# One scan over two channel halves in a selective-scan layer: a carry column between the halves, two two-bank decay buffers, one side bank

## The chip, the core and the metric

The kernel runs on one core of one Trainium2 chip. The metric is the device time of that core in microseconds, from the first to the last instruction. Five engines work from queues of their own: TensorE (PE in the profile, with PEld for its weight loads), VectorE (DVE), ScalarE (ACT), GpSimd (POOL) and SyncE (SP), which here only issues transfers. [...] a bank holds 512 float32 columns.

## The reference, cut to what matters

The program has two layers. The second (a Fourier attention block) is untouched by the change. The first is a two-dimensional selective scan: for each of 4 images of 48x48 pixels with 256 inner channels, four directions k run over the 2304 pixels, and each channel d has 16 states:

```python
def step(h, inp):
    dt_l, u_l, B_l, C_l = inp
    dA = jnp.exp(dt_l[..., None] * A)
    h = h * dA + (dt_l * u_l)[..., None] * B_l[:, :, None, :]
    y = jnp.einsum('bkdn,bkn->bkd', h, C_l)
    return (h, y)
```

Directions 2 and 3 run the pixels backwards. Afterwards come a sum over the directions, a layer norm over the channels, a multiplication by silu(z) and an output projection.

## The kernel before

Channels lie on the 128 partitions, so the 256 channels are two halves f = 0, 1 side by side in the free dimension. Pixels are cut into chunks of 480 (four of them, and one of 384) for each direction: 4 images x 4 directions x 5 chunks = 80 chunks. For every chunk the 16 states are 16 steps, 1280 steps in all. A step is spread over the engines:

```python
NX = 112
LC = 480
CHUNKS = [(s, min(LC, L - s)) for s in range(0, L, LC)]
...
three = ctx.enter_context(tc.tile_pool(name="l0_three", bufs=3))          # db, h, hc, cbc
ps_s = ctx.enter_context(tc.tile_pool(name="l0_pss", bufs=2, space=PSUM))  # side work
ps_b = ctx.enter_context(tc.tile_pool(name="l0_psb", bufs=1, space=PSUM))  # B of a state, spread
ps_a = ctx.enter_context(tc.tile_pool(name="l0_psa", bufs=3, space=PSUM))  # decays da
ps_y = ctx.enter_context(tc.tile_pool(name="l0_psy", bufs=1, space=PSUM))  # two sums yp
...
def drive_pool(u):          # every fourth step: the input term db on GpSimd
    u.db = three.tile([128, NF, LC], F32, tag="db", ...)
    if i % 4 == POOLS:
        nc.gpsimd.tensor_mul(u.db[:, :, 0:n], c.du[:, :, 0:n], u.bbc[...])
def spread(u):              # the other steps: TensorE spreads B over the partitions ...
    u.pb = ps_b.tile([128, 512], F32, tag="pb", ...)
    nc.tensor.matmul(u.pb[:, 0:n], pick[:, i : i + 1].to_broadcast([NX, 128]), c.bs[:, 0:n], ...)
def drive_in(u):            # ... and VectorE multiplies
    nc.vector.tensor_mul(u.db[:, :, 0:n], c.du[:, :, 0:n], u.pb[:, None, 0:n].to_broadcast(...))
def decay(u):               # ScalarE: exp(dt * A), one PSUM bank for each half
    for f in range(NF):
        da = ps_a.tile([128, 512], F32, tag="da", ...)
        nc.scalar.activation(da[:, 0:n], c.dt[:, f, 0:n], AF.Exp, scale=a_neg[:, q, i : i + 1])
        u.da.append(da)
def scan(u):                # VectorE: the recurrence, one scan for each half
    for f in range(NF):
        init = 0.0 if c.first else carry[:, i, f : f + 1]
        ...
        nc.vector.tensor_tensor_scan(ha, aa, ba, init, ALU.mult, ALU.add)
def read_out(u):            # GpSimd: times C
    nc.gpsimd.tensor_mul(u.hc[:, :, 0:n], u.h[:, :, 0:n], u.cbc.to_broadcast([128, NF, n]))
def carry_on(u):            # ScalarE: last column of both halves, for the next chunk
    nc.scalar.copy(carry[:, u.i], u.h[:, :, 0 if u.c.k >= 2 else u.c.n - 1])
def sum_up(u):              # TensorE: the sum over states, by the identity, in PSUM
    for f in range(NF):
        nc.tensor.matmul(c.yp[f][:, 0:n], ident, u.hc[:, f, 0:n], ...)
...
LAGS = (
    (0, fetch), (3, drive_pool), (4, drive_in), (5, scan), (4, decay), (5, read_out), (6, carry_on),
    (3, spread), (7, sum_up),
)
```

LAGS says how many steps after its fetch each stage of a step is recorded, and in which order within one advance. After each advance one piece of side work is recorded: the next direction's projections (`project`: TensorE into a side bank, ScalarE out of it), the next image's convolution (`front`) and the tail of finished chunks (`back`). A scheduling layer then orders each engine's queue; the queues are fixed when the program is built. `back` before the change, cut:

```python
pz = []
for f in range(NF):
    p = side(f"pz{t}_{f}")
    nc.tensor.matmul(like(p[:, 0:n], 1), w[...], xs, start=True, stop=True)
    pz.append(p)
for f in range(NF):
    nc.scalar.activation(z[:, f, 0:n], pz[f][:, 0:n], AF.Silu, bias=wb[...])
yield
nc.gpsimd.tensor_mul(ys, ys, z[:, :, 0:n])
yield
po = side(f"po{t}")
...   # two matmuls into po
yield
pr = side(f"pr{t}")
...   # three matmuls into pr
yield
nc.vector.tensor_mul(xo[:, 0:n], po[:, 0:n], rs[:, 0:n])
yield
nc.vector.tensor_add(xo[:, 0:n], xo[:, 0:n], pr[:, 0:n])
```

Of the kernel before, what the change touches and what calls it, by code (L numbers as in the profile page):

```python
# [22 lines left out]
D = 256  # L23
NF = D // 128
N = 16
R = 8
K = 4
NX = 112
NH = 32

LC = 480
# [4 lines left out]
def layer0(ctx, tc, io, x1_dram):  # L36
# [17 lines left out]

# [13 lines left out]

    w_xp = const.tile([128, K, NF, NX], F32, name="w_xp")
    nc.gpsimd.memset(w_xp, 0.0)  # L70
# [35 lines left out]
    def side(name):  # L106
        return ps_s.tile([128, 512], F32, tag="pp", name=name)
# [7 lines left out]
    def like(ap, k):  # L115

        return ap if k % 2 == 0 else ap.rearrange("p (w h) -> p w h", h=T)
# [73 lines left out]
    def project(b, k, chunks, xc):  # L191
# [5 lines left out]
        for c in chunks:  # L197
# [49 lines left out]
    def back(b, s, n, yb, x, w, wb):  # L247


        t = f"{b}_{s}"  # L250
        xs = at(x, 1, s, n)[:, 0]
        pm = side(f"pm{t}")
        for f in range(NF):
            nc.tensor.matmul(pm[:, 0:n], lnmat, yb[:, f, 0:n], start=(f == 0), stop=(f == NF - 1))
        yield
        ys = yb[:, :, 0:n]
        nc.vector.tensor_sub(ys, ys, pm[:, None, 0:n].to_broadcast([128, NF, n]))
        yield
# [12 lines left out]
        pz = []  # L271
        for f in range(NF):
            p = side(f"pz{t}_{f}")
            nc.tensor.matmul(
                like(p[:, 0:n], 1), w[:, D + f * 128 : D + (f + 1) * 128], xs, start=True, stop=True
            )
# [9 lines left out]
        yield  # L286
        pr = side(f"pr{t}")
# [4 lines left out]
        nc.vector.tensor_mul(xo[:, 0:n], po[:, 0:n], rs[:, 0:n])  # L292
        yield
# [5 lines left out]
    carry = const.tile([128, N, NF], F32, name="carry")  # L299

    class Chunk:


        def __init__(self, b, k, s, n, first, number, im):
            self.b, self.k, self.s, self.n, self.first, self.number, self.im = b, k, s, n, first, number, im
            self.t = f"{b}_{k}_{s}"

    class Step:
# [15 lines left out]
    def drive_pool(u):  # L324

        c, i, n = u.c, u.i, u.c.n
        u.db = three.tile([128, NF, LC], F32, tag="db", name=f"db{c.t}_{i}")
        if i % 4 == POOLS:
            nc.gpsimd.tensor_mul(u.db[:, :, 0:n], c.du[:, :, 0:n], u.bbc[:, :, 0:n].to_broadcast([128, NF, n]))  # L329

    def spread(u):

# [10 lines left out]
    def drive_in(u):  # L343
        c, i, n = u.c, u.i, u.c.n
        if i % 4 != POOLS:
            nc.vector.tensor_mul(  # L346
                u.db[:, :, 0:n], c.du[:, :, 0:n], u.pb[:, None, 0:n].to_broadcast([128, NF, n])
            )

    def decay(u):  # L350
        c, i, n = u.c, u.i, u.c.n
        u.da = []
        for f in range(NF):
            q = c.k * NF + f
            da = ps_a.tile([128, 512], F32, tag="da", name=f"da{c.t}_{i}_{f}")
            nc.scalar.activation(da[:, 0:n], c.dt[:, f, 0:n], AF.Exp, scale=a_neg[:, q, i : i + 1])  # L356
            u.da.append(da)

    def scan(u):
        c, i, n = u.c, u.i, u.c.n  # L360
        u.h = three.tile([128, NF, LC], F32, tag="h", name=f"h{c.t}_{i}")
        for f in range(NF):
            init = 0.0 if c.first else carry[:, i, f : f + 1]
            ha, aa, ba = u.h[:, f, 0:n], u.da[f][:, 0:n], u.db[:, f, 0:n]
            if c.k >= 2:
                ha, aa, ba = ha[:, ::-1], aa[:, ::-1], ba[:, ::-1]
            nc.vector.tensor_tensor_scan(ha, aa, ba, init, ALU.mult, ALU.add)  # L367

    def read_out(u):
        c, i, n = u.c, u.i, u.c.n  # L370
        u.hc = three.tile([128, NF, LC], F32, tag="hc", name=f"hc{c.t}_{i}")
        nc.gpsimd.tensor_mul(u.hc[:, :, 0:n], u.h[:, :, 0:n], u.cbc.to_broadcast([128, NF, n]))  # L372

    def carry_on(u):
        nc.scalar.copy(carry[:, u.i], u.h[:, :, 0 if u.c.k >= 2 else u.c.n - 1])  # L375

    def sum_up(u):

# [49 lines left out]
    def drain(gen):  # L428
        while gen in later:
            piece()  # L430
# [15 lines left out]
    images = [{} for _ in range(B)]  # L446
    directions = []
    for b in range(B):
        for k in ORDER:
            parts = CHUNKS if k < 2 else CHUNKS[::-1]  # L450
            directions.append(
                [
                    Chunk(b, k, s, n, i == 0, len(directions) * len(parts) + i, images[b])
                    for i, (s, n) in enumerate(parts)
                ]
            )
# [13 lines left out]
    for j, chunks in enumerate(directions):  # L470
        b, k = chunks[0].b, chunks[0].k
        if k == ORDER[-1]:
            if b + 1 < B:
                drain(coming)
            images[b]["x"] = load_x(b, "xr")
        nxt = upcoming(j + 1) if j + 1 < len(directions) else None
        for m, c in enumerate(chunks):
            if k == ORDER[0] and b + 1 < B and m == 2:
# [643 lines left out]
```

## Time and profile before

| what | value |
|---|---|
| device time, three runs | 6529.45, 6544.07 and 6547.69 us, median 6544.07 us |
| span of the profiled execution | 6527.3 us |
| first layer's steps, from the first input term to the last scan | 133 us to 4419 us |
| busy there (4286 us): DVE, POOL, PE, ACT | 3841.7, 3822.9, 3535.1, 2574.7 us |
| what follows (second layer, mostly) | 4419 us to 6527 us |

How to read the rows of the profile: L367 is line 367 of the kernel; after it come the engine, the operation, the tile written and the tiles read, the shape, and the count. Then follow the busy time in us, the mean duration of one instruction in ns, and the time for which the engine stood idle just before such instructions, with the instruction that ended most of that idle time. A duration may overlap the next instruction's start on the same engine, so the distance between two starts can be shorter than the duration.

### The profile page before, as it was taken

To read this page: it belongs to the slowest core of one execution; us is meant where nothing else is said; L and a number is where in the kernel's file an instruction comes from. 1 tells how busy PE (TensorE), PEld (TensorE's weight loads), DVE (VectorE), ACT (ScalarE), POOL (GpSimd) and SP (SyncE) were. 2 spreads that over 40 slices of the span, in tenths; PEclk is the share of its full clock that TensorE was granted. 3 is DMA by queue.
4 is the path that set the end of the run, shared out by engine and by line. 5 is a ranking of instruction groups with operands and counts; after the bars stand their busy time and mean duration, and the time that the engine had idled before them with its cause. 6 is when DMAs were issued, how large, how long until landed. Compare 5 with 4: busy or idle time off the path is not lost. (4 is left out here: it accounts for less than half of the span.)

```text
span 6527.3 us, 45804 instructions
## 1 busy us (share of the span) xinstructions
PE 4892.4 (75%) x12490; PEld 2172.5 (33%) x12490; DVE 5348.1 (82%) x5060; ACT 3047.5 (47%) x5657; POOL 4906.7 (75%) x2784
## 2 busy tenths in 40 slices
PE   7798878889877889887888777785233398878763
PEld 3343233334323334322333322332122244435332
DVE  1988889988989998888999898994699999963444
ACT  3656556655656665655666655553000133322222
POOL 2989889888999898888989999882565489951222
PEclk9999899999999999988999999997565655556876
DMA  1222233223223332233323323322200100010222
GB/s 39 89 89 93 89 92 96 89 92 93 94 92 90 96 97 88 93 92 88 94 92 104 92 95 93 90 93 50 53 1 0 16 8 4 4 40 8 59 59 58
DMA packets 271781, 457.67 MB, mean 70 GB/s; under 512 B 87134, under 2 KB 196734, under 8 KB 271522
## 3 DMA queue, kind: packets, MB, share of 16 engines
q1 hardware_dynamic: 224546, 438.13, 22.5%
q10 hardware_dynamic: 46976, 16.61, 1.4%
q8 instruction: 98, 1.61, 0.1%
q14 instruction: 161, 1.32, 0.1%
HBM read 419.60 MB, written 35.02 MB: 70 GB/s over the span
## 5 line engine op out<-in xcount | busy, mean ns | idle before, releaser
L372 POOL TENSOR_TENSOR hc<-h,cbc 128x960 f32<-128x960 f32 (+1 forms) x1280 | 2724.5, 2140 | 412.2 <-DVE h L367 237.1
L391 PE MATMUL yp<-hc,ident 128*128 128x480 f32 (+1 forms) x5120 | 2438.7, 599 | 570.8 <-POOL hc L372 566.5
L367 DVE TENSOR_TENSOR_SCAN h<-da,carry,db 128x480 f32<-128x480 f32 (+1 forms) x2048 | 2301.6, 1175 | 59.0 <-ACT da L356 22.1
L356 ACT ACTIVATE da<-dt,a_neg 128x480 f32<-128x480 f32 (+1 forms) x2560 | 1639.3, 647 | 1384.0 <-DVE h L367 1364.1
L391 PEld LDWEIGHTS yp<-hc,ident 128*128 128x128 f32 x5120 | 985.9, 202 | 1983.8 <-POOL hc L372 1089.4
L346 DVE TENSOR_TENSOR db<-du,pb 128x960 f32<-128x960 f32 (+1 forms) x960 | 1052.2, 1096 | 400.1 <-PE pb L339 353.8
L329 POOL TENSOR_TENSOR db<-du,bbc 128x960 f32<-128x960 f32 (+1 forms) x320 | 685.2, 2141 | 0.3
L887 PE MATMUL py<-attn_t,xt 48*128 48x384 f32 x768 | 507.7, 845 | 78.6 <-DVE m L895 71.8
L367 DVE TENSOR_TENSOR_SCAN h<-da,db 128x384 f32<-128x384 f32 (+1 forms) x512 | 505.4, 1038 | 27.1 <-ACT da L356 21.3
L339 PE MATMUL pb<-bs,pick 112*128 112x480 bf16 (+1 forms) x960 | 364.6, 380 | 140.5 <-DVE db L346 139.0
L889 ACT COPY ysb<-py 128x384 f32<-128x384 f32 x384 | 183.5, 478 | 404.8 <-PE py L887 360.9
L887 PEld LDWEIGHTS py<-attn_t,xt 48*128 48x128 f32 x768 | 233.6, 320 | 339.8 <-issue 149.3
L176 PE MATMUL pc<-pad,cdiag 128*128 128x480 f32 (+1 forms) x720 | 294.1, 550 | 0.0
L375 ACT COPY carry<-h 128x2 f32<-128x2 f32 x1280 | 227.8, 178 | 3.8 <-DVE h L367 2.5
L807 PE MATMUL pat<-ident,s 48*48 48x48 f32 x128 | 13.3, 277 | 274.5 <-POOL s L803 274.5
L204 PE MATMUL px<-xc,w_xp 128*112 128x480 f32 (+1 forms) x320 | 211.0, 770 | 4.7 <-ACT dt L229 2.7
L245 POOL TENSOR_TENSOR du<-dt,xc 128x480 f32<-128x480 f32 (+1 forms) x160 | 202.4, 1287 | 8.8 <-DVE db L346 4.4
L900 POOL TENSOR_TENSOR zi<-zi,m 128x384 f32<-128x384 f32 x192 | 191.8, 999 | 14.5
L898 POOL TENSOR_TENSOR zi<-gw,ysb 128x384 f32<-128x384 f32 x192 | 181.8, 947 | 25.7 <-ACT ysb L889 25.3
L899 POOL TENSOR_TENSOR m<-gw,ysb 128x384 f32<-128x384 f32 x192 | 185.2, 965 | 10.8 <-ACT ysb L889 10.8
L339 PEld LDWEIGHTS <-pick 112*128 112x128 bf16 x960 | 98.7, 103 | 273.5 <-issue 254.7
L389 PE MATMUL yp<-y,ident 128*128 128x480 f32 (+1 forms) x240 | 169.6, 824 | 20.9 <-ACT y L406 20.7
(263 smaller groups left out, 5804.9 us busy)
## 6 DMA issues: line engine op xcount, KB each, us to landing
cbc<-cd SPq DMA_DIRECT2D x512, 480.0 KB
bbc<-cd SPq DMA_DIRECT2D x256, 240.0 KB
cbc<-cd SPq DMA_DIRECT2D x128, 384.0 KB
bbc<-cd SPq DMA_DIRECT2D x64, 192.0 KB
da_wM<-a_wM SPq DMA_DIRECT2D x12, 396.0 KB
x<-in_xT SPq DMA_DIRECT2D x16, 288.0 KB
xr<-in_xT SPq DMA_DIRECT2D x16, 288.0 KB
e_wM<-de_wM SPq DMA_DIRECT2D x12, 384.0 KB
```

Of the source, the lines that this page charges most:

```text
L176: nc.tensor.matmul(pc[:, 0:n].rearrange("p (r c) -> p r c", c=H), cdiag[:, j], pad[:, r0 + dy : r0 + dy + nr, dx : dx + H], start=(j == 0) ...
L204: nc.tensor.matmul(like(px[0:NX, 0:n], k), w_xp[:, k, f], src[:, f], start=(f == 0), stop=(f == NF - 1))
L245: nc.gpsimd.tensor_mul(like(c.du[:, f, 0:n], c.k), like(c.dt[:, f, 0:n], c.k), src[:, f])
L329: nc.gpsimd.tensor_mul(u.db[:, :, 0:n], c.du[:, :, 0:n], u.bbc[:, :, 0:n].to_broadcast([128, NF, n]))
L339: nc.tensor.matmul(u.pb[:, 0:n], pick[:, i : i + 1].to_broadcast([NX, 128]), c.bs[:, 0:n], start=True, stop=True)
L346: nc.vector.tensor_mul(u.db[:, :, 0:n], c.du[:, :, 0:n], u.pb[:, None, 0:n].to_broadcast([128, NF, n]))
L356: nc.scalar.activation(da[:, 0:n], c.dt[:, f, 0:n], AF.Exp, scale=a_neg[:, q, i : i + 1])
L367: nc.vector.tensor_tensor_scan(ha, aa, ba, init, ALU.mult, ALU.add)
L372: nc.gpsimd.tensor_mul(u.hc[:, :, 0:n], u.h[:, :, 0:n], u.cbc.to_broadcast([128, NF, n]))
L375: nc.scalar.copy(carry[:, u.i], u.h[:, :, 0 if u.c.k >= 2 else u.c.n - 1])
L391: nc.tensor.matmul(c.yp[f][:, 0:n], ident, u.hc[:, f, 0:n], start=False, stop=(i == N - 1))
L887: nc.tensor.matmul(p[:, 0 : HG * T], xt[:, c, j], attn_t[:, b, hs], start=True, stop=True)
```

## The change

The two scans of a step become one. Its operands are laid out so that the two halves touch, parted by a single column: in the decays that column is 0, and in the input term it holds the carry of the half that is scanned second. At that column the recurrence gives h = 0 * h_before + carry, so the second half starts from its own carry. The first half's carry is the scan's initial value, as before.

- The decays of a step need 2n + 1 neighbouring columns, so `da` is now one tile of two PSUM banks, and there are two of them, used in turn: four banks in place of three. Half 0 ends at column 510, column 511 is the zero, and half 1 begins at column 512, in the second bank.
- The banks add up to eight again by taking one side bank away (two become one). The tail `back` is cut so that no two side tiles live at once: each `pz` is emptied by a ScalarE copy with its bias before the next is written, silu is applied to both in SBUF, and `po` is consumed before `pr` is written.
- ScalarE gets one more copy in every step, which sets the carry column. The carry tile exists twice, one for each direction in turn, and GpSimd sets it to zero at a direction's start; the copy of the last column is left out in a direction's last chunk.
- `db` and `h` have a pitch of n + 1 between the halves; their readers and writers use views through `halves`.

```diff
-    ps_s = ctx.enter_context(tc.tile_pool(name="l0_pss", bufs=2, space=PSUM))
+    ps_s = ctx.enter_context(tc.tile_pool(name="l0_pss", bufs=1, space=PSUM))
-    ps_a = ctx.enter_context(tc.tile_pool(name="l0_psa", bufs=3, space=PSUM))
+    ps_a = ctx.enter_context(tc.tile_pool(name="l0_psa", bufs=1, space=PSUM))
...  (back)
-        pz = []
         for f in range(NF):
-            p = side(f"pz{t}_{f}")
+            pz = side(f"pz{t}_{f}")
...
-            pz.append(p)
-        for f in range(NF):
-            nc.scalar.activation(z[:, f, 0:n], pz[f][:, 0:n], AF.Silu, bias=wb[:, NF + f : NF + f + 1])
+            yield
+            nc.scalar.activation(z[:, f, 0:n], pz[:, 0:n], AF.Identity, bias=wb[:, NF + f : NF + f + 1])
+            yield
+        nc.scalar.activation(z[:, :, 0:n], z[:, :, 0:n], AF.Silu)
...  (the multiplication of po by rs moves ahead of pr)
+    das = [ps_a.tile([128, 2 * BANK], F32, name=f"da{j}") for j in range(2)]
+    for da in das:
+        nc.vector.memset(da[:, BANK - 1 : BANK], 0.0)
+    carries = [const.tile([128, N, NF], F32, name=f"carry{j}") for j in range(2)]
+    def halves(ap, n):
+        return ap[:, 0 : 2 * (n + 1)].rearrange("p (f n) -> p f n", f=NF)[:, :, 0:n]
...  (decay)
-            da = ps_a.tile([128, 512], F32, tag="da", name=f"da{c.t}_{i}_{f}")
-            nc.scalar.activation(da[:, 0:n], c.dt[:, f, 0:n], AF.Exp, scale=a_neg[:, q, i : i + 1])
-            u.da.append(da)
+            o = BANK if f else BANK - 1 - n
+            nc.scalar.activation(u.da[:, o : o + n], c.dt[:, f, 0:n], AF.Exp, scale=a_neg[:, q, i : i + 1])
+        nc.scalar.copy(u.db[:, n : n + 1], c.carry[:, i, 1 - c.rev : 2 - c.rev])
...  (scan)
-        for f in range(NF):
-            init = 0.0 if c.first else carry[:, i, f : f + 1]
-            ha, aa, ba = u.h[:, f, 0:n], u.da[f][:, 0:n], u.db[:, f, 0:n]
-            if c.k >= 2:
-                ha, aa, ba = ha[:, ::-1], aa[:, ::-1], ba[:, ::-1]
-            nc.vector.tensor_tensor_scan(ha, aa, ba, init, ALU.mult, ALU.add)
+        m = 2 * n + 1
+        ha, aa, ba = u.h[:, 0:m], u.da[:, BANK - 1 - n : BANK + n], u.db[:, 0:m]
+        if c.rev:
+            ha, aa, ba = ha[:, ::-1], aa[:, ::-1], ba[:, ::-1]
+        nc.vector.tensor_tensor_scan(ha, aa, ba, c.carry[:, i, c.rev : c.rev + 1], ALU.mult, ALU.add)
...  (carry_on)
-        nc.scalar.copy(carry[:, u.i], u.h[:, :, 0 if u.c.k >= 2 else u.c.n - 1])
+        if not c.final:
+            nc.scalar.copy(c.carry[:, u.i], halves(u.h, c.n)[:, :, 0 if c.rev else c.n - 1])
...  (start of a direction)
+        nc.gpsimd.memset(carries[j % 2], 0.0)
```

LAGS and every other stage are as before; so is the second layer, whose queues hold the same instructions in the same order in both kernels.

More of the change, by code (lines that the diff above doesn't have):

```diff
@@ L28 @@
 NX = 112
+BANK = 512
 NH = 32
@@ L270, in back @@
         yield
-        pz = []
         for f in range(NF):
-            p = side(f"pz{t}_{f}")
+            pz = side(f"pz{t}_{f}")
             nc.tensor.matmul(
-                like(p[:, 0:n], 1), w[:, D + f * 128 : D + (f + 1) * 128], xs, start=True, stop=True
+                like(pz[:, 0:n], 1), w[:, D + f * 128 : D + (f + 1) * 128], xs, start=True, stop=True
             )
-            pz.append(p)
-        for f in range(NF):
-            nc.scalar.activation(z[:, f, 0:n], pz[f][:, 0:n], AF.Silu, bias=wb[:, NF + f : NF + f + 1])
+            yield
+            nc.scalar.activation(z[:, f, 0:n], pz[:, 0:n], AF.Identity, bias=wb[:, NF + f : NF + f + 1])
+            yield
+        nc.scalar.activation(z[:, :, 0:n], z[:, :, 0:n], AF.Silu)
         yield
@@ L286, in back @@
         yield
+        nc.vector.tensor_mul(xo[:, 0:n], po[:, 0:n], rs[:, 0:n])
+        yield
         pr = side(f"pr{t}")
@@ L291, in back @@
         yield
-        nc.vector.tensor_mul(xo[:, 0:n], po[:, 0:n], rs[:, 0:n])
-        yield
         nc.vector.tensor_add(xo[:, 0:n], xo[:, 0:n], pr[:, 0:n])
@@ L298, in layer0, with __init__ @@
     NQ = 2
-    carry = const.tile([128, N, NF], F32, name="carry")
+    das = [ps_a.tile([128, 2 * BANK], F32, name=f"da{j}") for j in range(2)]
[4 more added lines that the diff above has]
+        return ap[:, 0 : 2 * (n + 1)].rearrange("p (f n) -> p f n", f=NF)[:, :, 0:n]
     class Chunk:
-        def __init__(self, b, k, s, n, first, number, im):
-            self.b, self.k, self.s, self.n, self.first, self.number, self.im = b, k, s, n, first, number, im
+        def __init__(self, b, k, s, n, first, final, number, im):
+            self.b, self.k, self.s, self.n, self.number, self.im = b, k, s, n, number, im
+            self.first, self.final, self.rev = first, final, int(k >= 2)
             self.t = f"{b}_{k}_{s}"
@@ L326, in drive_pool @@
         c, i, n = u.c, u.i, u.c.n
-        u.db = three.tile([128, NF, LC], F32, tag="db", name=f"db{c.t}_{i}")
+        u.db = three.tile([128, NF * (LC + 1)], F32, tag="db", name=f"db{c.t}_{i}")
         if i % 4 == POOLS:
-            nc.gpsimd.tensor_mul(u.db[:, :, 0:n], c.du[:, :, 0:n], u.bbc[:, :, 0:n].to_broadcast([128, NF, n]))
+            nc.gpsimd.tensor_mul(halves(u.db, n), c.du[:, :, 0:n], u.bbc[:, :, 0:n].to_broadcast([128, NF, n]))
     def spread(u):
@@ L346, in drive_in @@
             nc.vector.tensor_mul(
-                u.db[:, :, 0:n], c.du[:, :, 0:n], u.pb[:, None, 0:n].to_broadcast([128, NF, n])
+                halves(u.db, n), c.du[:, :, 0:n], u.pb[:, None, 0:n].to_broadcast([128, NF, n])
             )
@@ L351, in decay @@
         c, i, n = u.c, u.i, u.c.n
[L352 removed]
+        u.da = das[i % 2]
         for f in range(NF):
             q = c.k * NF + f
[L355 to L357 removed]
+            o = BANK if f else BANK - 1 - n
+            nc.scalar.activation(u.da[:, o : o + n], c.dt[:, f, 0:n], AF.Exp, scale=a_neg[:, q, i : i + 1])
+        nc.scalar.copy(u.db[:, n : n + 1], c.carry[:, i, 1 - c.rev : 2 - c.rev])
     def scan(u):
         c, i, n = u.c, u.i, u.c.n
[L361 to L367 removed]
+        u.h = three.tile([128, NF * (LC + 1)], F32, tag="h", name=f"h{c.t}_{i}")
+        m = 2 * n + 1
[3 more added lines that the diff above has]
+        nc.vector.tensor_tensor_scan(ha, aa, ba, c.carry[:, i, c.rev : c.rev + 1], ALU.mult, ALU.add)
     def read_out(u):
@@ L371, in read_out @@
         u.hc = three.tile([128, NF, LC], F32, tag="hc", name=f"hc{c.t}_{i}")
-        nc.gpsimd.tensor_mul(u.hc[:, :, 0:n], u.h[:, :, 0:n], u.cbc.to_broadcast([128, NF, n]))
+        nc.gpsimd.tensor_mul(u.hc[:, :, 0:n], halves(u.h, n), u.cbc.to_broadcast([128, NF, n]))
     def carry_on(u):
-        nc.scalar.copy(carry[:, u.i], u.h[:, :, 0 if u.c.k >= 2 else u.c.n - 1])
+        c = u.c
+        if not c.final:
+            nc.scalar.copy(c.carry[:, u.i], halves(u.h, c.n)[:, :, 0 if c.rev else c.n - 1])
     def sum_up(u):
@@ L452, in layer0 @@
                 [
-                    Chunk(b, k, s, n, i == 0, len(directions) * len(parts) + i, images[b])
+                    Chunk(b, k, s, n, i == 0, i == len(parts) - 1, len(directions) * len(parts) + i, images[b])
                     for i, (s, n) in enumerate(parts)
@@ L476, in layer0 @@
         nxt = upcoming(j + 1) if j + 1 < len(directions) else None
+        nc.gpsimd.memset(carries[j % 2], 0.0)
         for m, c in enumerate(chunks):
+            c.carry = carries[j % 2]
             if k == ORDER[0] and b + 1 < B and m == 2:
```

## The prediction, made before the changed kernel ran

> **What bounds the kernel now.** I read the busy time of each engine in two stretches first (us from the span's start; PE, PEld, DVE, ACT, POOL busy with instruction counts, granted clock, DMA share, GB/s):
>
> ```profile
> 133.00:4419.00 4286.00, 3535.13 (x8065) 1451.31 (x8064) 3841.72 (x3632) 2574.70 (x4882) 3822.93 (x1988) 0.94 0.30 92
> ```
>
> The change touches only this stretch. VectorE is busy for 3842 of 4286 us (89.6%), GpSimd for 3823 us (89.2%): two engines at the same load, neither full. What each waits for, in the same window, says how they are tied (who waited for whom: us in total, times, longest):
>
> ```profile
> ACT da L356 <- DVE h L367: 1364.1, 1663, 6.8
> ...
> PE yp L391 <- POOL hc L372: 566.2, 422, 4.6
> DVE db L346 <- PE pb L339: 353.8, 209, 5.9
> ...
> POOL hc L372 <- DVE h L367: 237.1, 216, 4.7
> ...
> POOL hc L372 <- PE yp L391: 107.7, 66, 3.8
> ```
>
> ScalarE waits for the scans, not the other way round. VectorE's one large wait is for the spread B (354 us in 209 waits); TensorE has it late because, in its queue, it stands behind sums that wait for GpSimd's product `hc`. GpSimd in turn waits 237 us for scans. So this is a pair of equal stages with few buffers between them, which stall each other by turns.
>
> Then the scans' own rows, with shapes kept apart (count | busy us, mean ns of one | idle before):
>
> ```profile
> L372 POOL TENSOR_TENSOR hc<-h,cbc 128x960 f32<-128x960 f32 x1024 | 2263.0, 2222 | 309.6 <-DVE h L367 209.6 <-PE yp L391 57.2 <-PE pb L339 14.2
> L367 DVE TENSOR_TENSOR_SCAN h<-da,carry,db 128x480 f32<-128x480 f32 x1792 | 2058.5, 1199 | 48.6 <-ACT da L356 22.1 <-POOL hc L372 11.7 <-ACT carry L375 0.5
> ...
> L367 DVE TENSOR_TENSOR_SCAN h<-da,db 128x480 f32<-128x480 f32 x256 | 278.4, 1138 | 21.9 <-ACT da L356 21.3
> L367 DVE TENSOR_TENSOR_SCAN h<-da,carry,db 128x384 f32<-128x384 f32 x256 | 243.1, 1000 | 10.3 <-ACT carry L375 5.7
> ...
> L367 DVE TENSOR_TENSOR_SCAN h<-da,db 128x384 f32<-128x384 f32 x256 | 227.0, 938 | 5.2 <-ACT xd L209 0.5
> ```
>
> A mean is not what a scan takes from the queue, since the next one starts before it has ended. The timeline of VectorE shows the distance (start us, length us, xcount):
>
> ```profile
> 1008.27 3.43 DVE L367 TENSOR_TENSOR_SCAN h<-da,carry,db 128x480 f32<-128x480 f32 x3
> 1011.62 1.13 DVE L346 TENSOR_TENSOR db<-du,pb 128x960 f32<-128x960 f32 x1
> 1012.66 3.43 DVE L367 TENSOR_TENSOR_SCAN h<-da,carry,db 128x480 f32<-128x480 f32 x3
> ```
>
> Three scans of 480 take 3.43 us, so two distances are 3.43 - 1.20 = 2.23 us: one each 1.115 us. An input term takes 1.04 us (1011.62 to 1012.66). Three scans of 384 elsewhere take 2.83 us, so their distance is (2.83 - 1.00) / 2 = 0.915 us. The slope is (1115 - 915) / 96 = 2.08 ns a column and the fixed part 1115 - 480 x 2.08 = 115 ns.
>
> [...] 2.08 ns a column, while `db` of 960 and of 768 columns (1135 and 939 ns) differ by 1.02 ns a column. So merging scans can't save on columns, only on the fixed part. [...] here it is 115 ns, with PSUM as a source and a carry read from SBUF. [...] Before, ScalarE could refill one half after half a step: its timeline shows exponentials 1.11 us apart (1004.12, 1005.23, 1006.34 us), each released by one scan.
>
> **The change part by part.**
>
> 1. One scan of 961 columns takes 115 + 961 x 2.08 = 2117 ns of the queue's time, in place of 2 x 1115 = 2230: 113 ns less. With 769 columns it is 1717 in place of 1830, again 113. That is one fixed part less two ns for the extra column. It holds for the 1024 steps with a carry: 116 us. In a direction's first chunk (256 steps) the initial value was a constant, and such scans were 61 ns shorter (1199 - 1138); the merged scan now reads a zero carry, so 2 x 1054 = 2108 becomes 2117: 2 us lost. **Part 1: -114 us of VectorE's queue.**
>
> 2. ScalarE gets 1280 single-column copies. The present two-column copy takes 178 ns: at most 228 us more on an engine that is busy for 2575 of 4286 us, so not a bound. But the scan now waits for both exponentials and the copy. From scan i-2's end ScalarE needs 0.66 + 0.58 us for two exponentials (the mean is 0.66; neighbours of 384 columns, 0.58 long, stand 0.08 us closer than that in the timeline) and about 0.2 us for two small copies, 1.5 us in all; VectorE spends at least one scan of 2.1 us in between, and mostly an input term of 1.04 us too. That fits. I laid the built queues of both kernels side by side: in 136 of 1280 steps ScalarE's queue puts the next step's exponential ahead of this step's second one, so that this scan needs an exponential that waits for the scan just before it. Such a scan starts about 1.4 us after the last one (two exponentials and the hand-over), where the input term between them fills 1.04: about 0.4 us each, 136 x 0.4 = **54 us**. Before there was one such case.
>
> 3. The order of VectorE's queue: in 81 places (16 before) an input term now needs a spread B that must wait for the input term just ahead of it, because the one `pb` bank is still being read. That costs the matmul of 0.38 us and two hand-overs, about 0.5 us: 65 x 0.5 = **32 us**.
>
> 4. TensorE's queue: of the 2560 sums, 1521 (1288 before) need no VectorE work later than their own scan. So 18% fewer sums are held up (1039 in place of 1272), which should loosen the two waits on TensorE that I read above, 354 and 108 us. 18% of their sum is 83 us; I take half, since I know the order and not the lengths: **-40 us**.
>
> 5. One side bank: 77 matmuls of `pd` now wait for ScalarE to empty the bank they share with their neighbour, and 20 of `pz` likewise. They are spaced by a step each, so I expect little: 97 x 0.15 us, **+15 us**. `back` has four more pieces for 20 chunks, and 16 fewer table loads are built in (262 in place of 278, 1.28 us each, on ScalarE, which isn't the bound): nothing.
>
> 6. Second layer: the same queues, nothing.
>
> On VectorE's side the sum is -114 + 54 + 32 - 40 + 15 = -53 us. How much of it reaches the end depends on GpSimd. A full chunk needs there 20 products at 2.2 us, two `du` at 1.33 and two small subtractions at 1.09: 48.8 us. VectorE needs 32 x 1.115 + 12 x 1.04 = 48.2 us, and 16 x 2.117 + 12 x 1.04 = 46.4 us after. Measured is 4286 us over 64 + 16 x 0.8 = 76.8 full chunks, 55.8 us each. GpSimd's floor doesn't move. Since the pair is at 48 of 55.8 us, a faster VectorE gives slack and not a new pace; I keep all of the 53 us, because 40 of them come from waits on both sides. **Predicted: 6544 - 54 = 6490 us.**
>
> **Rivals.** (a) VectorE alone sets the pace, and the new waits vanish in slack: then parts 1 and 4 count whole, 114 + 83 us, and the time is 6350. For it: VectorE is the busiest engine; against it: GpSimd is within 19 us of it. (b) GpSimd sets the pace: then only the waits of GpSimd matter (237 us for scans, 108 us for TensorE), and the time stays within 20 us of 6544. Its 89% busy and the 48.8 us a chunk speak for this; that it waits for scans at all speaks against. (c) ScalarE becomes a link in every step: two exponentials and two copies can't begin before the scan two steps back has ended, and side work of 0.5 to 1 us often lies between them. If half of the steps lose 0.3 us, that is 190 us: 6680. Against it: 1.5 us must fit in 3.1 us, and ScalarE waits 1364 us for scans today. (d) The single side bank holds TensorE up, and with it sums, `hc` buffers and GpSimd: 97 stalls of 1.5 us would cost 145 us, 6600.
>
> **Range and chances.** The known gain is small (114 us is 1.7%) and the known losses are as large as what is left. Range 6390 to 6590: the low end is rival (a) with half of part 4 (6544 - 114 - 40), the high end is (d) with most of part 1 taken off again (6544 + 145 - 100). Over 2% faster means below 6413, for which nearly all of (a) must come true: 0.16. Over 2% slower means above 6675, which needs (c): 0.05. Within 2%: 0.79.
>
> **What would show it.** A merged scan with a mean near 2.2 us and a distance of 2.1 us (part 1); the wait of scans for exponentials up from 43 us to around 100 (part 2); the wait of input terms for the spread B between 280 and 350 us (parts 3 and 4); TensorE waiting for ScalarE at `pd` and `pz` by some 15 us (part 5); GpSimd busy for the same 3823 us, with a higher share (b). I am wrong if the scan's fixed part turns out larger across two banks, if the scans' wait for ScalarE goes past 150 us, or if the wait for the spread B falls below 200 us.

## The result and the profile after

The changed kernel takes 6643.47 us (median of four runs, 6639.22 to 6644.92), the kernel before 6541.4 us in the runs beside it: 1.0157 times the time, interval 1.014 to 1.0175. It is **slower by 1.6%, or 103 us** (1.57% of 6541 us). The prediction was 6490 us with a range up to 6590, so it missed, on the hopeful side.

The stretch of the steps comes first again (us; busy time and count of PE, PEld, DVE, ACT and POOL, granted clock, DMA share, GB/s). It now begins at 160 us, not 133, and ends at 4511:

```profile
160.00:4511.00 4351.00, 3588.02 (x8057) 1461.25 (x8056) 3764.11 (x2350) 2597.98 (x5908) 3813.24 (x2000) 0.93 0.29 91
```

VectorE is busy for 78 us less than before (3764.1, was 3841.7), as the change intends, yet the stretch is 65 us longer (4351, was 4286). It also starts 27 us later, and 18 us more follow it (2126.3 after the last scan, was 2108.5). So VectorE stands idle for 143 us more: 587, was 444. The waits in this window (who waited for whom: us in total, times, longest) give part of the answer:

```profile
ACT da L368 <- DVE h L378: 1173.2, 822, 5.6
...
DVE db L358 <- PE pb L351: 367.8, 264, 6.7
...
POOL hc L383 <- DVE h L378: 161.1, 113, 5.6
...
ACT dt L230 <- PE pd L220: 135.6, 50, 7.7
...
POOL hc L383 <- issue: 121.7, 77, 6.0
ACT db L369 <- POOL db L341: 110.9, 53, 6.3
DVE h L378 <- ACT db L369: 71.5, 69, 9.8
...
DVE h L378 <- ACT da L368: 52.5, 26, 4.8
```

The rows of the kernel before, from its own window (133 to 4419 us), that belong beside them:

```profile
DVE h L367 <- ACT da L356: 43.4, 17, 6.0
...
POOL hc L372 <- issue: 21.8, 11, 3.4
...
ACT dt L229 <- PE pd L219: 18.8, 17, 2.7
```

Three rows are new or have grown. The scans wait 137 us for ScalarE in all (71.5 for the carry column, 52.5 for exponentials and 12.7 for the carry copy), where it was 50. ScalarE waits 136 us for the projection `pd`, where it was 19. And ScalarE's single-column copy waits 111 us for GpSimd's input term, although it writes another column of the tile. The wait for the spread B is 368 us, no smaller than before (354). GpSimd is busy for the same time as before (3813, was 3823). The row of its waits for scans has shrunk (161, was 237), but this is the view's doing: of the 122 us under "issue" (was 22), 121 us end 0.13 us after the end of the product's own scan. Counted by that end (a product that starts within 0.26 us of it), GpSimd waits for scans for 391 us, where it was 280.

By groups (count | busy us, mean ns of one | idle before, and who ended it), the scan itself is what the prediction worked out:

```profile
L378 DVE TENSOR_TENSOR_SCAN h<-da,carry,db 128x961 f32<-128x961 f32 x1024 | 2238.2, 2209 | 106.6 <-ACT da L368 33.6 <-ACT db L369 22.1 <-ACT carry L388 10.9
...
L378 DVE TENSOR_TENSOR_SCAN h<-da,carry,db 128x769 f32<-128x769 f32 x256 | 455.2, 1808 | 76.2 <-ACT db L369 49.4 <-ACT da L368 18.9 <-POOL hc L383 5.5
```

Its rows are busy for 2238.2 + 455.2 = 2693 us, where the four rows before sum to 2807: 114 us less. But two thirds of the wait for the column copy lie ahead of the 256 short scans. From the starts of the first scans of all 80 chunks, the 64 chunks of 480 take 3527 us in all, as before (3531); the 16 chunks of 384 take 824 us, 68 more than before (755).

One place of the timeline (start us, length us, engine, line; in brackets the idle time before it and who ended it) shows how the engines then hold each other up:

```profile
884.40 0.61 PE L351 MATMUL pb<-bs,pick 112*128 112x480 bf16 x1
...
885.04 1.16 DVE L358 TENSOR_TENSOR db<-du,pb 128x960 f32<-128x960 f32 x1 [0.90 <-PE pb L351]
885.06 0.66 ACT L368 ACTIVATE da<-dt,a_neg 128x480 f32<-128x480 f32 x1
...
885.70 3.57 PE L404 MATMUL yp<-hc,ident 128*128 128x480 f32 x4 [0.69 <-POOL hc L383]
886.11 2.21 DVE L378 TENSOR_TENSOR_SCAN h<-da,carry,db 128x961 f32<-128x961 f32 x1
...
889.20 1.96 PE L220 MATMUL pd<-xd,w_dt 8*128 8x480 f32 x2
...
891.09 0.58 PE L351 MATMUL pb<-bs,pick 112*128 112x480 bf16 x1
891.20 0.66 ACT L230 ACTIVATE dt<-pd,b_dt 128x480 f32<-128x480 f32 x1 [5.48 <-PE pd L220]
...
891.71 1.16 DVE L358 TENSOR_TENSOR db<-du,pb 128x960 f32<-128x960 f32 x1 [3.38 <-PE pb L351]
891.76 0.66 ACT L368 ACTIVATE da<-dt,a_neg 128x480 f32<-128x480 f32 x1
...
892.78 4.32 DVE L378 TENSOR_TENSOR_SCAN h<-da,carry,db 128x961 f32<-128x961 f32 x2
```

TensorE runs the two sums of a step (each is recorded as two matmuls), then the `pd` of half 1, then the next spread B. ScalarE has come to the emptying of that `pd` and waits 5.48 us for it, with the next exponential behind it in its queue. VectorE waits 3.38 us for the spread B, which comes after `pd` on TensorE. No engine is short of work elsewhere; each is held by the order of its queue. The last row gives the scan's distance: 4.32 - 2.21 = 2.11 us, predicted 2.117.

### The profile page after: what moved, and what is told of

Read it like the earlier page. It is cut to its first block, busy times and chain, and to the rows that moved or that the text cites. A ratio compares the mean times of both kernels' runs of the same rounds, so it can differ in the third digit from the quotient of the medians.

```text
span 6637.4 us, 45081 instructions
## 1 busy us (share of the span) xinstructions
PE 4965.0 (75%) x12490; PEld 2185.8 (33%) x12490; DVE 5272.1 (79%) x3782; ACT 3072.4 (46%) x6685; POOL 4899.6 (74%) x2800
## 5 line engine op out<-in xcount | busy, mean ns | idle before, releaser
L404 PE MATMUL yp<-hc,ident 128*128 128x480 f32 (+1 forms) x5120 | 2482.9, 609 | 568.8 <-POOL hc L383 556.3
L378 DVE TENSOR_TENSOR_SCAN h<-da,carry,db 128x961 f32<-128x961 f32 (+1 forms) x1280 | 2693.3, 2129 | 182.8 <-ACT db L369 71.5
L404 PEld LDWEIGHTS yp<-hc,ident 128*128 128x128 f32 x5120 | 1002.1, 206 | 1984.5 <-POOL hc L383 1103.7
L369 ACT COPY db<-carry 128x1 f32<-128x1 f32 x1280 | 228.7, 182 | 152.1 <-POOL db L341 110.9
L220 PE MATMUL pd<-xd,w_dt 8*128 8x480 f32 (+1 forms) x320 | 179.3, 642 | 13.3 <-ACT dt L230 10.1
L388 ACT COPY carry<-h 128x2 f32<-128x2 f32 x1024 | 186.7, 182 | 0.5
```

The costliest lines, as they stand in the source:

```text
L369: nc.scalar.copy(u.db[:, n : n + 1], c.carry[:, i, 1 - c.rev : 2 - c.rev])
L378: nc.vector.tensor_tensor_scan(ha, aa, ba, c.carry[:, i, c.rev : c.rev + 1], ALU.mult, ALU.add)
L404: nc.tensor.matmul(c.yp[f][:, 0:n], ident, u.hc[:, f, 0:n], start=False, stop=(i == N - 1))
```

## The experiments

Two explanations stood against each other at first. **The side bank**: taking one side bank away (with the tail cut to fit it) costs more than the merged scan gives. **The merged scan**: its longer chain on ScalarE (two exponentials and a copy) and its two-bank buffers cost VectorE its gain. Ratios are against the kernel before, run on the same chip beside each experiment, with 95% intervals. A difference between two experiments is taken from their ratios, with 1% as 65.4 us.

### What the side bank costs

**Two scans, one side bank.** The kernel before, with the new tail and nothing else of the change:

```diff
-    ps_s = ctx.enter_context(tc.tile_pool(name="l0_pss", bufs=2, space=PSUM))
+    ps_s = ctx.enter_context(tc.tile_pool(name="l0_pss", bufs=1, space=PSUM))
```

> Two scans a step as before, three decay banks as before; only the side pool has one bank and the tail of a chunk is recorded as in the changed kernel. Theory S (the single side bank is paid where nothing runs beside it: before the first scan and after the last): first scan at about 160 us in place of 133, 18 us more after the last scan, 6541 + 45 = 6586 us. Theory C (the loss lies in the copies of the carry column): no change, 6541. If the single bank also holds up sums in the middle: above 6600.

Measured: 6665.15 us, ratio 1.0208 (1.0193 to 1.0224). Without the merged scan the kernel is slower still, so the side bank and the tail cost more than the whole loss. The waits from the first scan to the last:

```profile
DVE db L346 <- PE pb L339: 427.3, 282, 5.7
POOL hc L372 <- DVE h L367: 317.5, 231, 4.6
...
ACT dt L229 <- PE pd L219: 198.1, 46, 8.4
```

ScalarE's 46 waits for `pd` (4.3 us each) take 198 us, and the input terms wait 73 us longer for the spread B than before. The late start is explained too. In the kernel before, TensorE runs each half of the first image's convolution without a break:

```profile
33.19 35.06 PE L176 MATMUL pc<-pad,cdiag 128*128 128x480 f32 x90
```

With one side bank, each chunk waits for ScalarE to empty it:

```profile
50.47 7.51 PE L176 MATMUL pc<-pad,cdiag 128*128 128x480 f32 x18 [0.75 <-ACT xc L185]
58.73 7.51 PE L176 MATMUL pc<-pad,cdiag 128*128 128x480 f32 x18 [0.75 <-ACT xc L185]
```

The first scan starts at 158.8 us in place of 132.9: 26 us lost before any step has run.

**The new tail with two banks.** The same kernel with `bufs=2` for the side banks, so that only `back` differs from before:

> The kernel before, with only the tail of a chunk recorded as in the changed kernel; side banks stay two. If the single bank made e1 slow (138 us): about the time before, 6527 to 6545. If the longer tail (four more pieces for each of 20 chunks) made it slow: near e1's 6665, and the loss lies in the chunks of direction 3 and the start of the next image.

Measured: 6580.72 us, ratio 1.0058 (1.0043 to 1.0073): the tail alone costs 38 us. It lies mostly in the first direction of an image, where the tail of the image before is recorded (883 us before, 924 after, for those 16 chunks of 480). Two waits of the tail have grown, ScalarE's for `pz` and TensorE's for GpSimd's product of `yb` with `z`, which the tail now makes later:

```profile
ACT ws L277 <- PE pz L273: 82.9, 37, 6.2
...
PE po L285 <- POOL yb L281: 37.3, 18, 2.3
```

They were 11.0 and 8.7 us. That these waits are the cause is read, not tested. The first experiment over this one, 1.0208 / 1.0058 = 1.0149, is the price of the bank alone: 98 us.

**Two side banks with an owner each.** The new tail with two banks, but one serves `px` and `pd` only, the other everything else. If the cost of one bank comes from different users meeting in it, this must be nearly free of it:

```diff
-    ps_s = ctx.enter_context(tc.tile_pool(name="l0_pss", bufs=2, space=PSUM))
+    ps_s = ctx.enter_context(tc.tile_pool(name="l0_pss", bufs=1, space=PSUM))
+    ps_p = ctx.enter_context(tc.tile_pool(name="l0_psp", bufs=1, space=PSUM))
...
-            px = side(f"px{c.t}")
+            px = ps_p.tile([128, 512], F32, tag="pd", name=f"px{c.t}")
...
-                pd = side(f"pd{c.t}_{f}")
+                pd = ps_p.tile([128, 512], F32, tag="pd", name=f"pd{c.t}_{f}")
```

> The kernel before with the new tail (e5, 6581 us with two side banks in one pool); the two side banks are split, one for the projections alone and one for everything else. If the single bank costs because different users wait for each other: near e5's 6581. If it costs in the hand-over within one user (matmul, ScalarE's copy out, next matmul): near e1's 6665, with ScalarE's wait for pd near 200 us and the first scan near 159 us.

Measured: 6679.4 us, ratio 1.0222 (1.0204 to 1.0239), as slow as one bank, and the first scan is late too (156.7 us):

```profile
DVE db L347 <- PE pb L340: 458.2, 294, 5.8
...
ACT dt L230 <- PE pd L220: 209.0, 52, 8.4
```

So the loss lies in the hand-over within one user (`pd` of half 1 after `pd` of half 0, one convolution piece after the next), which two banks hide only if they are used in turn.

**More time between the hand-overs.** Exact tiles (below), plus one more pause after each `px` and each `pd`, so that their emptying is recorded a step later:

```diff
                 yield
+                yield
                 nc.scalar.activation(c.dt[:, f, 0:n], pd[:, 0:n], AF.Identity, bias=b_dt[:, k, f : f + 1])
```

> The changed kernel with exact tiles; in the projections one more piece lies between a matmul into the side bank and ScalarE's copy out of it. If ScalarE standing idle for pd (122 us) is how the single bank costs time in the middle: that wait falls by half or more and the time by 30 to 60 us, to 6550 to 6580. If that wait is hidden beside others: 6610.

Measured: 6611.04 us, ratio 1.011 (1.0093 to 1.0127), against 1.0121 without the pauses: no difference. ScalarE's wait for `pd` went up from 122 to 145 us. Recording it later does not bring it down; that the scheduling layer, which orders the queues, undoes it is my guess. Since the wait did not fall, the run does not say what the wait costs.

### What the merged scan gives and costs

**Tiles of exact size.** In a chunk of 384 the column copy waits for the multiplication into its own tile. For the short chunks the copies start only after it; for the long ones, some 810 of the 1024 start before it has ended. The columns written are not the same, but in a tile cut for 480 columns the scheduling layer seems to take the view of the two short halves and the single column between them as overlapping. The change with tiles cut to the chunk:

```diff
-        u.db = three.tile([128, NF * (LC + 1)], F32, tag="db", name=f"db{c.t}_{i}")
+        u.db = three.tile([128, NF * (n + 1)], F32, tag="db", name=f"db{c.t}_{i}")
...
-        u.h = three.tile([128, NF * (LC + 1)], F32, tag="h", name=f"h{c.t}_{i}")
+        u.h = three.tile([128, NF * (n + 1)], F32, tag="h", name=f"h{c.t}_{i}")
```

> The changed kernel, with db and h allocated at just 2 (n + 1) columns, by which the copy of the carry column in the chunks of 384 no longer waits for the multiplication that fills the same tile. Theory C: the 16 short chunks lose their 68 us again, 6643 - 68 = 6575, and the wait of the copies for GpSimd (111 us) and of the scans for the copies (72 us) falls to near zero. Theory S: the short chunks are slow for another reason, 6643.

Measured: 6610.39 us, ratio 1.0121 (1.0106 to 1.0136). The copies' idle time is gone (1.9 us in place of 152.1), the scans wait 21.9 us for them in place of 71.5, and the short chunks take 783 us in place of 824, which is some 40 of the 68 us that had been lost there:

```profile
L369 ACT COPY db<-carry 128x1 f32<-128x1 f32 x1280 | 227.1, 181 | 1.9 <-POOL carry L490 1.4
```

A false dependency was worth 0.36%, some 24 us. Against the two scans with one side bank, 1.0121 / 1.0208 = 0.9915, the merged scan gains some 57 us once it is rid of it. The chunks of 480 are 72 us shorter than there.

**The column copy earlier.** Exact tiles, with the copy recorded ahead of the step's multiplication instead of after its exponentials:

```diff
         u.db = three.tile([128, NF * (n + 1)], F32, tag="db", name=f"db{c.t}_{i}")
+        nc.scalar.copy(u.db[:, n : n + 1], c.carry[:, i, 1 - c.rev : 2 - c.rev])
...
-        nc.scalar.copy(u.db[:, n : n + 1], c.carry[:, i, 1 - c.rev : 2 - c.rev])
```

> The changed kernel with exact tiles; the copy of the carry column is recorded a step earlier, ahead of the exponentials. If the copies and the order of ScalarE's queue cost what the scans wait for ScalarE (77 us in e2): that wait falls below 50 us and the time by some 20 to 30 us, to 6585. If the pair is held elsewhere: 6610.

Measured: 6720.69 us, ratio 1.0274 (1.0258 to 1.0289), worse by 1.5%. The waits show what happened:

```profile
ACT db L340 <- DVE h L378: 1175.2, 855, 6.1
...
DVE db L359 <- PE pb L352: 466.0, 312, 5.8
...
DVE h L378 <- ACT da L369: 131.5, 96, 6.8
```

The copy must wait for the scan that frees its `db` buffer. Put in front of the exponentials, it carries that wait into ScalarE's queue, and exponentials whose buffer is free stand behind it. The scans' wait for ScalarE, which was to fall below 50 us, is 142.

**Decays in SBUF.** If `da` lies in SBUF, the merged scan needs no PSUM and the second side bank can stay:

```diff
-    ps_s = ctx.enter_context(tc.tile_pool(name="l0_pss", bufs=1, space=PSUM))
+    ps_s = ctx.enter_context(tc.tile_pool(name="l0_pss", bufs=2, space=PSUM))
...
-    das = [ps_a.tile([128, 2 * BANK], F32, name=f"da{j}") for j in range(2)]
+    das = [const.tile([128, 2 * BANK], F32, name=f"da{j}") for j in range(2)]
```

> The changed kernel, with the two decay buffers in SBUF in place of PSUM, and two side banks again. Theory S: 45 us come back, 6598; first scan at about 133 us. If reading two PSUM banks made the merged scan costly, its mean of 2209 ns falls and the time falls further; if ScalarE is slower into SBUF than into PSUM, its exponential of 661 ns grows and scans wait more for it.

> The two edits together. Theories S and C add: 6643 - 45 - 68 = 6530, about the time of the kernel before. If GpSimd sets the pace of the pair (rival b of the prediction) it does not go below 6520 although VectorE has 114 us less to do; if VectorE's gain counts in full, 6541 - 114 = 6430.

Measured: 8459.09 us, ratio 1.2953 (1.2933 to 1.2972), and with exact tiles 8445.5 us, 1.2934 (1.2912 to 1.2955). The front is back at 133 us, as the second side bank should bring. All else is swamped by something I had not thought of. The groups of the first of the two:

```profile
L382 POOL TENSOR_TENSOR hc<-h,cbc 128x960 f32<-128x960 f32 x1024 | 3389.3, 3331 | 231.6 <-DVE h L377 90.0 <-issue 55.6 <-PE yp L403 51.3
L377 DVE TENSOR_TENSOR_SCAN h<-da,carry,db 128x961 f32<-128x961 f32 x1024 | 3342.9, 3281 | 433.8 <-POOL hc L382 232.6 <-ACT db L368 68.5 <-ACT da L367 66.3
...
L357 DVE TENSOR_TENSOR db<-du,pb 128x960 f32<-128x960 f32 x768 | 870.8, 1134 | 416.8 <-PE pb L350 370.4 <-POOL du L245 42.7
```

The scan, whose sources now both come from SBUF, goes from 2209 to 3281 ns, and GpSimd's product from 2225 to 3331, while VectorE's other multiplication, with one source in PSUM, stays at 1134 (1140 in the changed kernel). Only the place of the decays and the second side bank differ from the changed kernel, so I read these numbers as scans and products that slow each other. A full chunk's 16 scans of 2.12 us and its 20 GpSimd products of 2.2 us, at the lengths they have with the decays in PSUM, make 78 us laid end to end; measured is (6345 - 133) / 76.8 = 80.9 us a chunk, no shorter than one after the other. By what means they slow each other is not shown. The experiment says nothing on the side bank in the steps. It does say that in this kernel, with GpSimd multiplying beside it, the scan is better off with one source in PSUM: 1.0157 times the time before, against 1.2953 with both in SBUF.

### Does VectorE's queue count at all?

**No carry.** The kernel before with a constant initial value in every scan (`init = 0.0`); it leaves out the carry between the chunks. Nominally 2048 scans become 61 ns shorter, 125 us, with no change to buffers:

> The kernel before with a constant zero as every scan's initial value: it leaves out the carry from chunk to chunk, and nothing else. The 2048 scans that read a carry become 61 ns shorter each, 125 us off VectorE alone; banks, tail and pools are as before. If a shorter VectorE counts in full: 6541 - 125 = 6416. If GpSimd sets the pace: 6541. If the pair shares it: about 6480.

Measured: 6424.04 us, ratio 0.983 (0.9812 to 0.9849), 110 us less than the kernel before beside it (6534.2).

```profile
L367 DVE TENSOR_TENSOR_SCAN h<-da,db 128x480 f32<-128x480 f32 x2048 | 2228.8, 1136 | 90.7 <-ACT da L356 49.2 <-POOL hc L372 20.2 <-issue 2.9
```

VectorE is busy for 118 us less from the first scan to the last (3723.5), and nearly all of it comes off the time, with GpSimd as busy as before (3816.6 us). So a saving on VectorE's queue does count, and GpSimd does not set the pace. The merged scan saves the same 114 us in its own rows and passes on 57 at most.

### What a PSUM bank is worth elsewhere

The wait for the spread B is the largest on VectorE in every kernel so far, and it has one bank. These runs give it more.

**Spread B in the side pool.** Exact tiles, `pb` taken from the side pool, which has two banks:

```diff
-    ps_s = ctx.enter_context(tc.tile_pool(name="l0_pss", bufs=1, space=PSUM))
-    ps_b = ctx.enter_context(tc.tile_pool(name="l0_psb", bufs=1, space=PSUM))
+    ps_s = ctx.enter_context(tc.tile_pool(name="l0_pss", bufs=2, space=PSUM))
...
-        u.pb = ps_b.tile([128, 512], F32, tag="pb", name=f"pb{c.t}_{i}")
+        u.pb = ps_s.tile([128, 512], F32, tag="pp", name=f"pb{c.t}_{i}")
```

> The changed kernel with exact tiles; the spread B and the side work now share one pool of two banks (the spread had a bank of its own, the side work one). If the single side bank is what costs: the wait of ScalarE for pd (122 us in e2) falls, first scan back near 133 us, and the time falls from 6610 towards 6610 - 138 + something, below 6541 if the merged scan's 55 us then stand alone (6480). If the spread then waits for side tiles to be emptied: the wait of db for pb rises above 379 us and the time stays at 6610 or above.

Measured: 6469.55 us, ratio 0.9885 (0.987 to 0.9899): by the two ratios 154 us (1.0121 - 0.9885) faster than the same kernel with one bank for each use, with the same eight banks. The wait for the spread B, 379 us there, is now:

```profile
DVE db L357 <- PE pb L350: 214.3, 161, 6.0
```

The first scan does not come back to 133 us (158.7). The convolution runs without a break again (74 matmuls in a row, 28.51 us), but in TensorE's queue the first spread B now stands behind nearly all projections of the first direction (with three shared banks, below, it begins 42 us after the convolution). Every run below that shares a pool starts late like this (159 to 163 us).

**The same with two scans.** The kernel before with the new tail and the same shared pool of two, so one bank fewer in use than before:

> The kernel before (two scans a step, three decay banks) with the new tail, and spread B and side work sharing one pool of two banks as in e6: it differs from e6 only in the scans, the decay buffers and the carry column. If the 114 us of VectorE that the merged scan saves count in full once the spread has two banks: 6470 + 114 = 6584. If GpSimd sets the pace: 6470 to 6500, the merged scan is worth little and the shared pool did it all. With the 57 us that the merged scan was worth between e1 and e2: 6527.

Measured: 6471.24 us, ratio 0.9893 (0.9877 to 0.9908). The merged scan is worth nothing here. From first to last scan its VectorE is busy for 91 us less (3745 and 3836), but idle for 78 us more (441 and 363); 52 of these are for the spread B (214 and 162), and 31 are for side results (83 and 52). That a longer scan lets results of TensorE come late more often, and frees `pb` in larger lumps, is my reading of these totals; no run isolates it. Its row for the spread B:

```profile
DVE db L345 <- PE pb L338: 162.3, 126, 3.7
```

**Two scans, one side bank, two banks for the spread B.**

```diff
-    ps_b = ctx.enter_context(tc.tile_pool(name="l0_psb", bufs=1, space=PSUM))
+    ps_b = ctx.enter_context(tc.tile_pool(name="l0_psb", bufs=2, space=PSUM))
```

> e1 (two scans, one side bank, new tail, 6665 us) with a second bank for the spread B alone. If e6 is faster than e2 because of the second spread buffer: the wait of db for pb falls from 427 to about 250 us and the time by about 140 us to 6525. If it is because the side work has two banks now and then: 6665, and ScalarE's wait for pd stays near 200 us.

Measured: 6546.78 us, ratio 1.001 (1.0002 to 1.0019), which is 130 us better (1.0208 - 1.001) than one bank each, and 77 us worse (1.001 - 0.9893) than the shared pool of two, which has one bank fewer.

```profile
ACT dt L229 <- PE pd L219: 218.3, 46, 8.4
...
DVE h L367 <- ACT da L356: 189.9, 119, 6.2
DVE db L346 <- PE pb L339: 154.5, 128, 4.5
```

The wait for the spread B falls by 273 us (from 427.3), but less than half of that reaches the end: ScalarE waits for `pd` as long as before, and the scans now wait 190 us for its exponentials (67 with one bank each).

**Two scans, three shared banks.** The kernel before with its own tail; the two side banks and the one of the spread B become one pool of three:

> The kernel before, tail included, with its two side banks and its spread bank put into one pool of three: the eight banks of before, only shared. If it is the second buffer of the spread B that helped e6: the wait of db for pb falls from 354 to about 200 us, and the time by 60 to 100 us to about 6460. If sharing helps only because e6 had too few banks: 6541 as before.

Measured: 6440.88 us, ratio 0.9843 (0.9828 to 0.9857). This is the best full version, faster than both kernels, with two scans, eight banks and three lines touched. The wait for the spread B is less than half of the 353.8 us before, while the scans wait longer for exponentials (113.0 us, was 43.4):

```profile
DVE db L345 <- PE pb L338: 152.7, 110, 4.0
POOL hc L371 <- DVE h L366: 136.1, 138, 3.6
...
DVE h L366 <- ACT da L355: 113.0, 93, 3.3
...
ACT dt L228 <- PE pd L218: 66.7, 47, 5.6
```

The steps take 4169 us (4286 before), and the late start gives 27 us of that back: TensorE's first spread B begins 42 us after the convolution, where it began 11 us after it (127.30 us).

```profile
79.92 35.08 PE L175 MATMUL pc<-pad,cdiag 128*128 128x480 f32 x90
...
157.10 0.58 PE L338 MATMUL pb<-bs,pick 112*128 112x480 bf16 x2
```

**No carry on top of it.** The constant initial value in this kernel (again the carry is left out):

> The same edit on e10 (one pool of three banks), which has fewer waits for the spread B. In full: 6441 - 125 = 6316. GpSimd: 6441. Shared: about 6380. A larger part than in e13 would say that the waits for the spread ate the saving.

Measured: 6336.69 us, ratio 0.9692 (0.9672 to 0.9712): 99 us less (0.9843 - 0.9692). VectorE's queue counts as much there.

**Less on GpSimd.** The merged scan with the shared pool of two, and only every eighth step's input term on GpSimd instead of every fourth, so that VectorE and TensorE get 160 more:

> e6 with every eighth input term on GpSimd in place of every fourth: GpSimd loses 160 x 2.2 = 352 us of work, VectorE gains 160 x 1.04 = 166 us. If GpSimd sets the pace of the pair: faster than e6's 6470, towards 6350. If VectorE does: slower, up to 6640. If they share it: within 40 us of 6470.

Measured: 6518.16 us, ratio 0.9968 (0.9948 to 0.9987), 54 us slower (0.9968 - 0.9885) than with every fourth. GpSimd sheds about 320 us (3476.5 busy) and the kernel gains nothing by it; VectorE is busy for 156 us more (3901), and a third of that reaches the end. VectorE stays the tighter of the two.

## Why the prediction was wrong

The measured steps add up along the chain of kernels, each against the one before it:

| step | us | predicted |
|---|---|---|
| new tail | +38 | 0 |
| one side bank in place of two | +98 (26 of it before the first scan) | +15 |
| merged scan, without the false dependency | -57 | -114 + 54 + 32 - 40 = -68 |
| false dependency in the chunks of 384 | +24 | not seen |
| together | +103 | -53 |

**Part 5 is the step that failed.** It put the side bank at 97 stalls of 0.15 us, an estimate with no measured stall behind it, and the tail at nothing; together they cost 136 us. The places were right and the reasoning was not: "spaced by a step each" asked how long TensorE would wait. TensorE does wait only some 13 us at `pd` and `pz` (9.5 + 0.7 and 1.8 + 1.1 in the rows of these matmuls), close to the 15 predicted. The cost falls on the other side: the second `pd` stands later in TensorE's queue, behind sums, and ScalarE, whose queue has the emptying next, idles 136 us (84 of them for the `pd` of half 1; in the run with two scans and one side bank 190 of 198). None of the prediction's three signs of being wrong appeared (a dearer scan, over 150 us of waits for ScalarE, under 200 us for the spread B): it had set none where the loss came. Rival (d) had the size right (145 us) and its chain partly: it saw TensorE held up and GpSimd after it, while the runs show ScalarE and the spread B. Put in place of part 5 in the prediction's own sum, its 145 us give 6544 - 68 + 145 = 6621 us, and not the 6600 stated. A second side bank, used in turn with the first, is worth 98 us in this kernel. The part also missed the front, where no step hides a hand-over: with one side bank TensorE stands idle for 0.75 us ahead of a chunk of the convolution, and the first scan comes 26 us late.

**Part 1** was right in the scan's distance (2.11, predicted 2.117) and in the 114 us of its rows. VectorE's whole busy time fell by 78 us only. Summed over the instructions of both traces, 34 us of the difference are overlap between scans and other instructions that is gone (127 us before, 93 after: where the next instruction has to wait, nothing covers a scan's end); the other rows are 2 us longer.

**Part 2** expected the scans' wait for ScalarE at around 100 us. It is 137, half of it from the carry column, and that half is mostly the false dependency that I did not look for. With exact tiles it is 78 (46.0 for exponentials, 21.9 for the column, 9.8 for the carry).

**Parts 3 and 4** predicted the wait for the spread B between 280 and 350 us; it is 368. The direction was right against its proper base: one side bank raises it from 354 to 427, and the merged scan with exact tiles brings it to 379, or -48, where parts 3 and 4 together said -8. With a shared pool the merged scan raises it instead (162 to 214). So the count of held-up sums does not predict this wait. The reading behind it, that the spread B is late because it stands behind sums, was at most part of it: with the pool of three, and nothing else changed in the program, the wait falls from 354 to 153 us. More than half of it went with the single bank.

**Part 6** said the second layer is the same. 18 us more follow the last scan. This stretch takes between 2108 and 2124 us in the profiles of the other kernels (2108.7 with one side bank, 2123.8 in the last run without a carry), so one profile of each does not tie the 18 us to the change. I leave this open.

**How much reaches the end.** I kept all of the VectorE sum, since the pair is at 48 of 55.8 us. That choice stands for a shorter scan (110 of 125 us without the carry). Rival (b) falls with that run, rival (a) with the merged scan itself. Rival (c), ScalarE a link in every step, is not what happened: the merged scan gains by itself, so the 1.5 us mostly fit.

Of the bank's 98 us, 72 lie in the steps. That they go through the hand-over of one user's two tiles is what the run with an owner for each bank says. How they split between ScalarE's wait and the later spread B is not settled.

## What to carry to other kernels

Before a PSUM bank is traded for fewer instructions, look for the tiles it lets overlap and ask what the reader's in-order queue does while it waits, not only the writer's. Here the tile that most steps wait for gained more from a pool of two shared with the side work (1.0208 to 0.9893) than from two banks of its own (1.0208 to 1.001). Merging two instructions saved their fixed part (two scans take 2.23 us of the queue, the merged one 2.11), but the unit that others wait for grew from 1.115 to 2.11 us, and with the shared pool nothing of the saving was left (6471.24 and 6469.55 us); a plain cut on the same queue (the constant initial value) passed on 99 and 110 us.

## What the runs showed of the hardware that I had not expected

- With both sources of the scan in SBUF, scans and GpSimd's multiplications beside them each took half as long again: 2209 to 3281 ns and 2225 to 3331 ns.
- Reading a scan's initial value from SBUF in place of a constant costs about 61 ns each time, and over 2048 scans those show up nearly in full in the kernel's time (110 of 125 us).
